# Summing the 32-wide squares of a causal channel attention on TensorE, by accumulating transposes

## The chip, the cores and the metric

The kernel runs on one core of a Trainium2 chip, in one launch. The metric is the device time of the whole launch in microseconds, as a median over runs.

## The reference, cut to what matters

The input x has 8 batches of 512 tokens with 256 features, all in 32-bit floats. Four layers follow each other, each with a layer norm ahead and a residual behind it: attention A, a feed-forward part, attention B (an ordinary causal attention over tokens) and the same feed-forward part again. The change lies in attention A, which attends, for each token and each of 16 heads, over the head's own 64 channels:

```python
Q = (x @ Wq + bq).reshape(b, s, H, C) * inv_sqrt_c      # H, C = 16, 64
K = (x @ Wk + bk).reshape(b, s, H, C)
V = (x @ Wv + bv).reshape(b, s, H, C)
scores = jnp.einsum('bshq,bshk->bshqk', Q, K)
mask = jnp.triu(jnp.ones((C, C), dtype=bool), 1)
scores = jnp.where(mask, -jnp.inf, scores)
w = jax.nn.softmax(scores, axis=-1)
attn = jnp.einsum('bshqk,bshk->bshq', w, V)
```

So for every token and head there is a lower triangle of 64 x 64 products q_i k_j, their exponentials, the sum of these over j (the denominator) and the sum of these times v_j (the numerator). None of this is a matmul over tokens: it is elementwise work with a token on each partition.

## The kernel before

**Squares.** A triangle of 64 is cut into one square of 32 x 32, two of 16, four of 8 and so on, and the diagonal. The kernel takes 128 tokens (i, of 4) of a batch (b, of 8) and 4 heads (g, of 4) at a time: 128 groups (b, g, i). The squares of a group are worked in four *units* (`units`, `NU = 4`): unit 0 has the squares of 32 of two heads, unit 2 those of the other two heads, unit 1 all squares of 16, and unit 3 all smaller ones. The loop runs over 512 *steps*, one unit each; `self.at(n - k)` names the unit that entered k steps ago, so a unit goes through a software pipeline of some ten steps.

**One unit's way.** `scores` (L804) forms the products of q and k: on POOL for units 0 and 2, on DVE for units 1 and 3. `exps` (L818, ACT) takes the exponential in place one step later. `weigh` (L828, DVE) multiplies by v into the other part of the same buffer, again one step later; so a buffer of 4096 columns holds 2048 exponentials (e) and 2048 weighted ones (ev). `halve` (L834) starts, from POOL's queue, a DMA that adds the upper 2048 columns onto the lower 2048. For the squares of 32 `fold` (L839, POOL) then adds 1024 columns onto 1024, `gather` (L865) reduces on DVE the remaining 8 columns of each row to one, and `add_rows` (L872, POOL) adds these 128 sums (e and ev of two squares, 32 rows each) to the accumulator `acc` of the group. Units 1 and 3 have no fold. Then `invert` (L876, DVE), `divide` (L880, POOL), `turn_group` (L888, PE transposes) and `project_out` (L896, PE) make the new x.

**Layout.** In `pieces` a buffer of unit 0 or 2 is laid out as (b a x i j): four blocks b of 8 columns, a for e or ev, x for the two squares, i for the 32 rows, and j, the 8 columns of a block, innermost. So each row's sum runs over neighbouring elements.

**Buffers.** The three buffers `w` of units 0 and 2 turn round. PSUM has eight banks; attention A has one of them, `bank`, in two halves of 256 columns, which `half_bank` hands out in turn to the transposes of x (L567), the product k (L761, copied away by L781), the transposed group (L888, copied by L738) and the output product (L896 to L491, copied by L907). q and v stay in another PSUM tile, `qv` (L766), from which DVE reads them.

**Order.** The order of PE, DVE, ACT and POOL is written out by hand: a step has three parts, and after each part the generator of the later layers (`after_a`: feed-forward L1072, L1140, L1166, attention B, feed-forward) of an earlier batch is advanced by as many pieces as the constant `total` allows. The engines run through their queues in program order. The later layers of the last batch remain when attention A is done; that is the tail.

These lines of `step` tell where the sums of a square of 32 are made, n being the present step:

```python
            b, i, g, u = self.at(n - 4)      # second part
            if u == 0:
                self.fold(b, i, g, u)
            b, i, g, u = self.at(n - 3)
            if u == 2:
                self.fold(b, i, g, u)
...
            b, i, g, u = self.at(n - 4)      # third part
            if u == 2:
                self.gather(b, i, g, u)
            b, i, g, u = self.at(n - 5)
            if u == 0:
                self.gather(b, i, g, u)
```

Of the kernel before, what the change touches and what calls it, by code (L numbers as in the profile page):

```python
# [16 lines left out]
P = 128  # L17
# [267 lines left out]
def fast_path(ctx: ExitStack, tc: tile.TileContext, k, t, flag):  # L285
# [214 lines left out]


    bank = ps_a.tile([P, 2, GW], F32, name="bank")
    halves = [0]

    def half_bank():
        halves[0] ^= 1
        return bank[:, halves[0], :]

    def judge():

# [72 lines left out]

    JB = 8

    def pieces(w, n, off, nsq, cols):

        def of_rows(v):
            return v[:, cols].rearrange("p (x t) -> p x t", t=2 * n)[:, :, n:]

        def of_cols(v):
            return v[:, cols].rearrange("p (x t) -> p x t", t=2 * n)[:, :, :n]

        if n < 16:
            e, ev = (
                w[:, a * SMALL + off : a * SMALL + off + nsq * n * n].rearrange("p (x i j) -> p x i j", i=n, j=n)  # L600
                for a in range(2)
            )
            yield e, ev, lambda v: of_rows(v).unsqueeze(3), lambda v: of_cols(v).unsqueeze(2)
            return
        both = w.rearrange("p (b a x i j) -> p a b x i j", a=2, x=nsq, i=n, j=JB)
        if n == 32:
            for x in range(nsq):
                yield (
                    both[:, 0, :, x],
                    both[:, 1, :, x],  # L610
                    lambda v, x=x: of_rows(v)[:, x].unsqueeze(1).unsqueeze(3),
                    lambda v, x=x: of_cols(v)[:, x].rearrange("p (b j) -> p b j", j=JB).unsqueeze(2),
                )
        else:
            for k in range(n // JB):
                yield (
                    both[:, 0, k],
                    both[:, 1, k],
                    lambda v: of_rows(v).unsqueeze(3),
                    lambda v, k=k: of_cols(v)[:, :, k * JB : (k + 1) * JB].unsqueeze(2),  # L620
                )

    class AttentionA:
# [33 lines left out]
        def step(self, n):  # L657

            weighed = self.at(n - 2)
            if weighed[0] is not None:  # L660
                self.weigh(*weighed)
            unit = self.at(n)
            on_pool = unit[3] in (0, 2)
            if on_pool:
                half = self.scores(*unit)
                next(half)
            if weighed[0] is not None:
                self.halve(*weighed)
            if on_pool:
                next(half, None)  # L670
            b, i, g, u = self.at(n + 40)
            if u == 0 and g == 0 and i == 0 and b > 0:
                self.x[b] = load_x(b)
            b, i, g, u = self.at(n + 10)
            if u == 0 and g == 0 and i == 0 and b > 0:
                self.measure(b)
            b, i, g, u = self.at(n + 8)
            if u == 0 and g == 0:
                self.live["xn"] = normed(self.x[b][:, i, :], *self.rn[b, i], "a")
            b, i, g, u = self.at(n - 5)  # L680
            if u == NU - 1:
                self.invert(b, i, g)
            b, i, g, u = self.at(n - 4)
            if u == 1:
                self.gather(b, i, g, u)
            b, i, g, u = self.at(n + 7)
            if u == 0 and g == 0:
                nc.scalar.copy(self.live[b, i], self.live.pop("ps_ln"))
            if self.at(n - 1)[0] is not None:
                self.exps(*self.at(n - 1))  # L690
            yield
            if unit[0] is not None and not on_pool:
                for _ in self.scores(*unit):
                    pass
            for args in self.sums:
                self.add_rows(*args)
            self.sums = []
            b, i, g, u = self.at(n - 5)
            if u == NU - 1:
                self.divide(b, i, g)  # L700
            b, i, g, u = self.at(n - 2)
            if u == NU - 1:
                self.small_squares(b, i, g)

            b, i, g, u = self.at(n - 4)
            if u == 0:
                self.fold(b, i, g, u)
            b, i, g, u = self.at(n - 3)
            if u == 2:
                self.fold(b, i, g, u)  # L710
            b, i, g, u = self.at(n - 9)
            if u == NU - 1:
                self.new_x(b, i, g)
            b, i, g, u = self.at(n + 2)
            if u == 0:
                self.keep_qk(b, i, g)
            b, i, g, u = self.at(n - 7)
            if u == NU - 1:
                self.turn_group(b, i, g)
            b, i, g, u = self.at(n - 8)  # L720
            if u == NU - 1:
                self.project_out(b, i, g)
            b, i, g, u = self.at(n + 3)
            if u == 0:
                self.project(b, i, g)
            yield
            b, i, g, u = self.at(n - 4)
            if u == 2:
                self.gather(b, i, g, u)
            b, i, g, u = self.at(n - 5)  # L730
            if u == 0:
                self.gather(b, i, g, u)
            b, i, g, u = self.at(n - 3)
            if u == NU - 1:
                self.gather(b, i, g, u)
            b, i, g, u = self.at(n - 7)
            if u == NU - 1:
                nc.scalar.copy(self.live["att"], self.live.pop("pta"))  # L738
            b, i, g, u = self.at(n + 8)
            if u == 0 and g == 0:  # L740
                self.live[b, i] = lnp.tile([P, DC, P], F32, tag="xnt_a", name=f"xnta_{b}_{i}", bufs=NT)
                self.live["ps_ln"] = turned_over(self.live.pop("xn"), half_bank().rearrange("p (c s) -> p c s", c=DC))
            yield

        def measure(self, b, tiles=range(NT)):
# [39 lines left out]
        def scores(self, b, i, g, n_u):  # L785

            qv, kt = self.live[b, i, g][:2]
            if n_u == 0:
                acc = ap_.tile([P, 2, GW], F32, tag="acc", name=f"acc_{b}_{i}_{g}", bufs=3)
                self.live[b, i, g].append(acc)  # L790
                nc.vector.tensor_tensor(acc[:, 0, :], qv[:, 0], kt[:, 0], ALU.mult)

            if n_u in (0, 2):
                w = wt.tile([P, 4096], F32, tag="w", name=f"w_{b}_{i}_{g}_{n_u}", bufs=3)
            elif n_u == 1:
                w = wt.tile([P, 4096], F32, tag="w16", name=f"w16_{b}_{i}_{g}")
            else:
                w = wt.tile([P, 2 * SMALL], F32, tag="ws", name=f"ws_{b}_{i}_{g}")
            self.live[b, i, g, n_u] = w
            eng, q = (nc.gpsimd, kt[:, 1]) if n_u in (0, 2) else (nc.vector, qv[:, 0])  # L800
            for n, off, nsq, cols in squares(units[n_u]):
                for e, ev, rows, columns in pieces(w, n, off, nsq, cols):
                    shape = list(e.shape)
                    eng.tensor_tensor(  # L804
                        e, rows(q).to_broadcast(shape), columns(kt[:, 0]).to_broadcast(shape), ALU.mult
                    )
                    yield

        def exps(self, b, i, g, n_u):
            w = self.live[b, i, g, n_u]  # L810
            if n_u == 0:
                acc = self.live[b, i, g][2]
                nc.scalar.activation(acc[:, 0, :], acc[:, 0, :], AF.Exp, scale=C**-0.5)
            if n_u < NU - 1:
                e = w.rearrange("p (b a r) -> p a b r", a=2, b=units[n_u][0][0] // JB)[:, 0]
            else:
                e = w[:, :SMALL]
            nc.scalar.activation(e, e, AF.Exp, scale=C**-0.5)  # L818
# [14 lines left out]
                w = self.live[b, i, g, n_u]  # L833
                nc.gpsimd.dma_start(w[:, :2048], w[:, 2048:], accum_op=ALU.add)  # L834

        def fold(self, b, i, g, n_u):

            w = self.live[b, i, g, n_u]
            nc.gpsimd.tensor_tensor(w[:, :1024], w[:, :1024], w[:, 1024:2048], ALU.add)  # L839

        def columns_of(self, w, n, off, nsq):

# [15 lines left out]
        def gather(self, b, i, g, n_u):  # L858


            w = self.live.pop((b, i, g, n_u))
            for n, off, nsq, cols in squares(units[n_u]):
                if n > 2:
                    red = ap_.tile([P, 2, nsq * n], F32, tag=f"red{nsq * n}", name=f"red_{b}_{i}_{g}_{n_u}_{n}", bufs=2 + (n < 32))
                    nc.vector.tensor_reduce(red, self.columns_of(w, n, off, nsq), AX.X, ALU.add)  # L865
                    self.sums.append((b, i, g, n, cols, red))

# [604 lines left out]
```

## Time and profile before

| what | value |
|---|---|
| time, median of 3 runs | 3989.1 us (3984.17 to 3989.51) |
| span of the profiled execution | 3990.8 us |
| PE, weight load (PEld) | 3039.9, 2055.2 us busy |
| DVE, ACT, POOL | 3375.9, 2341.3, 3077.9 us busy |
| DMA issues of `halve` | 384, 7.8 us median from issue to landing |
| mean granted TensorE clock | 0.849 |

The page gives no time of the profiled execution other than its span. The span lies 1.7 us above the median of the unprofiled runs, so the two are taken as one. Busy times are shares of work done, not of work that mattered; "idle before, releaser" in a group's row says how long the engine stood still just before these instructions and what ended that. POOL's DMA issues are not counted in its busy time. Weight loads overlap matmuls, and the ends of matmuls are modelled.

### The profile page before, as it was taken

Reading aid. Unit: us, or ns where it says so; the run is one execution under the profiler, and the core shown is the slowest. Engines: PE = TensorE matmul, PEld = TensorE weight load, DVE = VectorE, ACT = ScalarE, POOL = GpSimd, SP = SyncE. Lnnn points to the kernel's source line nnn. Section 1 sums busy time; section 2 is a strip of 40 time slices with the busy share of each in tenths; the row PEclk is TensorE's granted clock in tenths of the full one; section 3 lists DMA queues with packets and bytes.
Section 4 is the critical chain, followed back from the end, with each engine's and each line's share of the span. In section 5 each row is a group of like instructions: output and inputs, shape, how many; then the busy total and the mean of one; then the engine's idle time right before and its main releaser. Section 6 shows DMA issues by size and latency. Waiting matters only on the chain.

```text
span 3990.8 us, 37932 instructions
## 1 busy us (share of the span) xinstructions
PE 3039.9 (76%) x12464; PEld 2055.2 (52%) x12464; DVE 3375.9 (85%) x3776; ACT 2341.3 (59%) x3156; POOL 3077.9 (77%) x3040
## 2 busy tenths in 40 slices
PE   5653487687877878678876878778787778778988
PEld 2231264365634656356643656346553556446847
DVE  7999988998899888998899988998989888996115
ACT  3444475576665675666755766666755767565342
POOL 6888878887888788887788887887888877886111
PEclk7556599798987988888987989879898889879999
DMA  8766777577776877768775877668776677767304
GB/s 229 182 137 137 159 197 158 124 191 189 199 154 139 196 191 178 148 163 202 200 157 118 208 186 194 149 142 213 174 190 143 160 182 206 158 129 211 116 28 169
DMA packets 118346, 669.24 MB, mean 168 GB/s; under 512 B 12662, under 2 KB 31865, under 8 KB 43643
## 3 DMA queue, kind: packets, MB, share of 16 engines
q0 software_dynamic: 78336, 570.46, 63.2%
q1 hardware_dynamic: 39804, 96.27, 6.7%
q8 instruction: 101, 1.65, 0.2%
q14 instruction: 105, 0.86, 0.1%
HBM read 254.07 MB, written 9.96 MB: 66 GB/s over the span
## 4 chain that ended last, share of the span: by engine, by line
DVE 38%; PE 18%; POOL 14%; DMA 13%; ACT 8%; issue 8%; SPq 0%; ACTq 0%; POOLq 0%; DVEq 0%
DVE red L865 15%; DMA w<-w 13%; DVE w L828 10%; PE ph L1140 5%; ACT w L818 4%; POOL w L804 3%; POOL w L839 3%; DVE ws L828 3%; PE pqkb L1187 3%; POOL acc L872 3%; DVE w L804 2%; DVE ws L804 2%; POOL h L1056 2%; POOL w L834 2%; DVE acc L876 2%
## 5 line engine op out<-in xcount | busy, mean ns | idle before, releaser
L818 ACT ACTIVATE w<-w 128x2048 f32<-128x2048 f32 x384 | 733.8, 1912 | 659.2 <-POOL w L804 461.3
L1140 PE MATMUL ph<-h,hidden 128*128 128x512 f32 x4096 | 1042.9, 411 | 72.4 <-POOL h L1056 42.9
L804 POOL TENSOR_TENSOR w<-k 128x1024 f32<-128x1024 f32 x512 | 1077.4, 2104 | 7.7 <-ACT k L782 7.1
L1140 PEld LDWEIGHTS ph<-h,hidden 128*128 128x128 f32 x4096 | 792.3, 195 | 275.3 <-POOL h L1056 53.8
L828 DVE TENSOR_TENSOR w<-w,qv 128x1024 f32<-128x1024 f32 x768 | 898.8, 1211 | 22.4 <-ACT w L818 22.4
L865 DVE TENSOR_REDUCE red<-w 128x128 f32<-128x1024 f32 (+1 forms) x384 | 601.3, 1566 | 178.0 <-DMA w<-w 93.6
L839 POOL TENSOR_TENSOR w<-w 128x1024 f32<-128x1024 f32 x256 | 643.7, 2514 | 82.9 <-DMA w<-w 82.3
L834 POOL DMA_DIRECT2D w<-w x384 | 337.9, 880 | 349.0 <-issue 121.1
L872 POOL TENSOR_TENSOR acc<-acc,red 128x256 f32<-128x256 f32 (+1 forms) x640 | 471.2, 736 | 142.7 <-DVE red L865 122.0
L865 DVE TENSOR_REDUCE red<-ws 128x256 f32<-128x2048 f32 (+1 forms) x256 | 435.4, 1742 | 0.0
L766 PE MATMUL qv<-wqv,xnta 128*128 128x512 f32 x512 | 299.7, 716 | 104.6 <-DVE ws L828 95.4
L1072 PE MATMUL pw<-xnt,gate 128*128 128x512 f32 (+2 forms) x1152 | 301.8, 422 | 21.7 <-ACT silu L1048 16.1
L828 DVE TENSOR_TENSOR ws<-ws,qv 128x1024 f32<-128x1024 f32 (+3 forms) x512 | 294.3, 635 | 27.6 <-ACT ws L818 27.6
L804 DVE TENSOR_TENSOR w<-qv,k 128x1024 f32<-128x1024 f32 x256 | 301.1, 1218 | 3.6
L804 DVE TENSOR_TENSOR ws<-qv,k 128x1024 f32<-128x1024 f32 (+3 forms) x512 | 299.5, 646 | 0.2 <-issue 0.2
L888 PE MATMUL bank<-ident,acc 128*128 128x128 f32 x256 | 62.4, 333 | 284.5 <-ACT k L781 278.6
L818 ACT ACTIVATE ws<-ws 128x1920 f32<-128x1920 f32 x128 | 231.5, 1808 | 80.7 <-DVE ws L804 80.1
L1072 PEld LDWEIGHTS pw<-xnt,gate 128*128 128x128 f32 x1152 | 230.8, 215 | 76.2 <-ACT silu L1048 20.4
L1249 ACT ACTIVATE eb<-psb 128x256 f32<-128x256 f32 (+3 forms) x512 | 182.1, 443 | 139.1 <-PE psb L1246 138.6
L1166 PE MATMUL pof<-w,h 128*128 128x256 f32 x1024 | 244.9, 392 | 22.8 <-ACT h L1105 22.8
L1105 ACT ACTIVATE h<-ph,s_sb 128x512 fp32r<-128x512 f32 (+1 forms) x256 | 171.2, 688 | 151.1 <-PE ph L1140 149.7
L876 DVE RECIPROCAL acc<-acc 128x256 f32<-128x256 f32 x128 | 222.9, 1741 | 11.9 <-POOL acc L872 11.9
(149 smaller groups left out, 4846.4 us busy)
## 6 DMA issues: line engine op xcount, KB each, us to landing
w<-w POOLq DMA_DIRECT2D x384, 1024.0 KB, 7.8
hidden<-in_h POOLq DMA_DIRECT2D x128, 1024.0 KB, 7.9
gate<-in_w12p POOLq DMA_DIRECT2D x32, 1024.0 KB, 9.1
w<-w_d SPq DMA_DIRECT2D x16, 1024.0 KB, 11.5
wqv<-wqv_d SPq DMA_DIRECT2D x31, 512.0 KB, 4.6
wo<-in_wo SPq DMA_DIRECT2D x32, 256.0 KB, 7.6
wbqk<-wbqk_d SPq DMA_DIRECT2D x8, 1024.0 KB, 9.0
w<-in_h SPq DMA_DIRECT2D x8, 1024.0 KB, 8.6
```

The lines of the kernel that those rows point to most:

```text
L766: nc.tensor.matmul(qv.rearrange("p j f -> p (j f)"), xnt[:, c, :], wqv[:, c, :], start=(c == 0), stop=(c == DC - 1),)
L804: eng.tensor_tensor(e, rows(q).to_broadcast(shape), columns(kt[:, 0]).to_broadcast(shape), ALU.mult)
L818: nc.scalar.activation(e, e, AF.Exp, scale=C**-0.5)
L828: nc.vector.tensor_tensor(ev, e, columns(qv[:, 1]).to_broadcast(list(e.shape)), ALU.mult)
L834: nc.gpsimd.dma_start(w[:, :2048], w[:, 2048:], accum_op=ALU.add)
L839: nc.gpsimd.tensor_tensor(w[:, :1024], w[:, :1024], w[:, 1024:2048], ALU.add)
L865: nc.vector.tensor_reduce(red, self.columns_of(w, n, off, nsq), AX.X, ALU.add)
L872: nc.gpsimd.tensor_tensor(rows, rows, part.rearrange("p a (x i) -> p a x i", i=n), ALU.add)
L876: nc.vector.reciprocal(acc[:, 0, :], acc[:, 0, :])
L1072: nc.tensor.matmul(pj[:, toks], w[:, m % 4, j, c, :], xs[:, p, c, toks], start=(p == 0 and c == 0), stop=(p == 1 and c == DC - 1),)
L1140: nc.tensor.matmul(pss[j], w[:, j, c, :], h_in(p, c), start=(p == 0 and c == 0), stop=(p == 1 and c == MC - 1),)
L1166: nc.tensor.matmul(po, h(0, c)[:, i * P : (i + 1) * P], w3[:, c, :], start=(c == 0), stop=False)
```

## The change

The squares of 32 are laid out as (j a x i): the column j outermost, and within one column 128 numbers, e and ev of two squares with 32 rows each. The halving DMA still adds 2048 columns onto 2048, which now leaves 16 columns j of 128 numbers each. Instead of fold, reduction and addition on POOL, TensorE transposes these 16 blocks of 128 x 128 one after the other into the same 128 columns of PSUM, with accumulation (`turn_sums`), ACT copies the sum to SBUF (`keep_sums`), TensorE transposes it back (`turn_sums_back`), and DVE adds it from PSUM to `acc` (`add_sums`). The second half of `bank` is kept for this; all other users share the first half. POOL still makes the products in two instructions (`parts=2`), and DVE's weighting of such a unit is one instruction instead of two. The tiles `red` of all widths now have three buffers.

```diff
     bank = ps_a.tile([P, 2, GW], F32, name="bank")
-    halves = [0]
     def half_bank():
-        halves[0] ^= 1
-        return bank[:, halves[0], :]
+        return bank[:, 0, :]
...
-    def pieces(w, n, off, nsq, cols):
+    def pieces(w, n, off, nsq, cols, parts=1):
...
-        both = w.rearrange("p (b a x i j) -> p a b x i j", a=2, x=nsq, i=n, j=JB)
         if n == 32:
-            for x in range(nsq):
+            both = w.rearrange("p (j a x i) -> p a j x i", a=2, x=nsq, i=n)
+            step = n // parts
+            for k in range(0, n, step):
                 yield (
-                    both[:, 0, :, x],
-                    both[:, 1, :, x],
-                    lambda v, x=x: of_rows(v)[:, x].unsqueeze(1).unsqueeze(3),
-                    lambda v, x=x: of_cols(v)[:, x].rearrange("p (b j) -> p b j", j=JB).unsqueeze(2),
+                    both[:, 0, k : k + step],
+                    both[:, 1, k : k + step],
+                    lambda v: of_rows(v).unsqueeze(1),
+                    lambda v, k=k: of_cols(v)[:, :, k : k + step].rearrange("p x j -> p j x").unsqueeze(3),
                 )
...
+            if self.at(n - 5)[3] in (0, 2):      # first part, ahead of exps
+                self.keep_sums()
...
-            if u == 0:
-                self.fold(b, i, g, u)      # at(n - 4), second part
-            if u == 2:
-                self.fold(b, i, g, u)      # at(n - 3), second part
+            if self.at(n - 5)[3] in (0, 2):      # second part, after keep_qk, ahead of turn_group
+                self.turn_sums_back()
...
-            if u == 2:
-                self.gather(b, i, g, u)    # at(n - 4), third part
-            if u == 0:
-                self.gather(b, i, g, u)    # at(n - 5), third part
+            b, i, g, u = self.at(n - 5)          # third part
+            if u in (0, 2):
+                self.add_sums(b, i, g, u)
...
+            b, i, g, u = self.at(n - 4)          # third part, last
+            if u in (0, 2):
+                self.turn_sums(b, i, g, u)
...
+        def turn_sums(self, b, i, g, n_u):
+            w = self.live.pop((b, i, g, n_u))
+            for j in range(16):
+                nc.tensor.matmul(
+                    bank[:, 1, :P], w[:, j * P : (j + 1) * P], ident,
+                    start=(j == 0), stop=(j == 15), is_transpose=True,
+                )
+        def keep_sums(self):
+            self.live["sums"] = ap_.tile([P, P], F32, tag="sums", name="sums")
+            nc.scalar.copy(self.live["sums"], bank[:, 1, :P])
+        def turn_sums_back(self):
+            nc.tensor.transpose(bank[:, 1, P:], self.live.pop("sums"), ident)
+        def add_sums(self, b, i, g, n_u):
+            ((n, h0, nh),) = units[n_u]
+            acc = self.live[b, i, g][2]
+            rows = acc[:, :, h0 * C : (h0 + nh) * C].rearrange("p a (x t) -> p a x t", t=2 * n)[..., n:]
+            nc.vector.tensor_tensor(
+                rows, rows, bank[:, 1, P:].rearrange("p (a x i) -> p a x i", a=2, i=n), ALU.add
+            )
```

More of the change, by code (lines that the diff above doesn't have):

```diff
@@ L604, in pieces @@
             return
-        both = w.rearrange("p (b a x i j) -> p a b x i j", a=2, x=nsq, i=n, j=JB)
         if n == 32:
-            for x in range(nsq):
+            both = w.rearrange("p (j a x i) -> p a j x i", a=2, x=nsq, i=n)
+            step = n // parts
+            for k in range(0, n, step):
                 yield (
-                    both[:, 0, :, x],
-                    both[:, 1, :, x],
-                    lambda v, x=x: of_rows(v)[:, x].unsqueeze(1).unsqueeze(3),
-                    lambda v, x=x: of_cols(v)[:, x].rearrange("p (b j) -> p b j", j=JB).unsqueeze(2),
+                    both[:, 0, k : k + step],
+                    both[:, 1, k : k + step],
+                    lambda v: of_rows(v).unsqueeze(1),
+                    lambda v, k=k: of_cols(v)[:, :, k : k + step].rearrange("p x j -> p j x").unsqueeze(3),
                 )
         else:
+            both = w.rearrange("p (b a x i j) -> p a b x i j", a=2, x=nsq, i=n, j=JB)
             for k in range(n // JB):
@@ L703, in step @@
                 self.small_squares(b, i, g)
-            b, i, g, u = self.at(n - 4)
-            if u == 0:
-                self.fold(b, i, g, u)
-            b, i, g, u = self.at(n - 3)
-            if u == 2:
-                self.fold(b, i, g, u)
             b, i, g, u = self.at(n - 9)
@@ L726, in step @@
             yield
-            b, i, g, u = self.at(n - 4)
-            if u == 2:
-                self.gather(b, i, g, u)
             b, i, g, u = self.at(n - 5)
-            if u == 0:
-                self.gather(b, i, g, u)
+            if u in (0, 2):
+                self.add_sums(b, i, g, u)
             b, i, g, u = self.at(n - 3)
@@ L801, in scores @@
             for n, off, nsq, cols in squares(units[n_u]):
-                for e, ev, rows, columns in pieces(w, n, off, nsq, cols):
+                for e, ev, rows, columns in pieces(w, n, off, nsq, cols, parts=2):
                     shape = list(e.shape)
@@ L813, in exps @@
                 nc.scalar.activation(acc[:, 0, :], acc[:, 0, :], AF.Exp, scale=C**-0.5)
-            if n_u < NU - 1:
+            if n_u in (0, 2):
+                e = w.rearrange("p (j a r) -> p a j r", a=2, j=32)[:, 0]
+            elif n_u == 1:
                 e = w.rearrange("p (b a r) -> p a b r", a=2, b=units[n_u][0][0] // JB)[:, 0]
@@ L834, in halve @@
                 nc.gpsimd.dma_start(w[:, :2048], w[:, 2048:], accum_op=ALU.add)
-        def fold(self, b, i, g, n_u):
-            w = self.live[b, i, g, n_u]
-            nc.gpsimd.tensor_tensor(w[:, :1024], w[:, :1024], w[:, 1024:2048], ALU.add)
+        def turn_sums(self, b, i, g, n_u):
+            w = self.live.pop((b, i, g, n_u))
+            for j in range(16):
+                nc.tensor.matmul(
+                    bank[:, 1, :P],
+                    w[:, j * P : (j + 1) * P],
+                    ident,
+                    start=(j == 0),
+                    stop=(j == 15),
+                    is_transpose=True,
+                )
[11 more added lines that the diff above has]
+            )
         def columns_of(self, w, n, off, nsq):
@@ L863, in gather @@
                 if n > 2:
-                    red = ap_.tile([P, 2, nsq * n], F32, tag=f"red{nsq * n}", name=f"red_{b}_{i}_{g}_{n_u}_{n}", bufs=2 + (n < 32))
+                    red = ap_.tile([P, 2, nsq * n], F32, tag=f"red{nsq * n}", name=f"red_{b}_{i}_{g}_{n_u}_{n}", bufs=3)
                     nc.vector.tensor_reduce(red, self.columns_of(w, n, off, nsq), AX.X, ALU.add)
```

## The prediction

> **What bounds the kernel now.** I read the busy shares and the chain of the page first, then windows cut at phase borders, then the waits inside one slow group, then the groups of the lines that the change touches.
>
> ```profile
> PE 3039.9 (76%) x12464; PEld 2055.2 (52%) x12464; DVE 3375.9 (85%) x3776; ACT 2341.3 (59%) x3156; POOL 3077.9 (77%) x3040
> ...
> DVE 38%; PE 18%; POOL 14%; DMA 13%; ACT 8%; issue 8%; SPq 0%; ACTq 0%; POOLq 0%; DVEq 0%
> ```
>
> VectorE leads both rows, but a share is a mean over phases. The starts of L791 (one per group of four steps, 128 in all) give a time per group: 23.7 us in the start-up, 24 to 26 while attention B runs, 26 to 35 while a feed-forward part runs. Cut there (start-up, eleven feed-forward groups, five attention-B groups, tail):
>
> ```profile
> 36.00:458.00 422.00, 215.62 (x443) 109.09 (x443) 409.25 (x423) 173.00 (x186) 358.55 (x313) 0.57 0.73 161
> ...
> 1233.70:1570.10 336.40, 270.33 (x1051) 203.47 (x1050) 294.27 (x343) 221.12 (x266) 272.70 (x278) 0.89 0.76 183
> 1570.10:1698.80 128.70, 94.89 (x488) 46.86 (x487) 120.25 (x125) 77.20 (x132) 110.77 (x99) 0.84 0.69 147
> ...
> 3618.00:3991.00 373.00, 339.70 (x1595) 254.41 (x1593) 126.44 (x154) 138.66 (x252) 89.46 (x125) 0.96 0.40 130
> ```
>
> Columns: length, then busy us of PE, weight load, DVE, ACT, POOL, then clock, DMA share, GB/s. DVE fills 97% of the start-up and 93% of attention B: it is the bound there. In the feed-forward stretch it is 87%, PE 80%, POOL 81%: nobody is full, so a loop of waits costs some 42 us of DVE idleness. The tail has no attention A left and is PE's. One feed-forward group (1512 to 1544) shows the loop:
>
> ```profile
> POOL w L839 <- DMA w<-w: 6.0, 1, 6.0
> DVE red L865 <- POOL w L839: 5.5, 1, 5.5
> ```
>
> The `fold` of unit 2 stands one step after its halving DMA; where feed-forward weights load too, the DMA is late, POOL stands at the fold, and DVE at the reduction behind it. Over the execution DVE waits 84.1 us for L839 and 93.6 us for DMA directly (unit 1's reduction, which the change leaves).
>
> **What the Trainium skill says.** "TensorE: Matmul & The Clock Gate", Part 4, says that a transpose is a matmul against identity, about 275 ns in a kernel, and that the clock gate does not open for it as for other matmuls. Lengths agree (L888: 270 to 449 ns); whether sixteen in a row hold the clock down no trace here shows. The same page, Part 2, says that only weight loads are pulled ahead, matmuls stay in program order: so a waiting transpose holds all feed-forward work behind it. "PSUM — Partial Sum Buffer", Terms, says that two engines may not be in one bank and quadrant at once. The trace agrees that the bank is guarded as a whole: L888 waits 278.6 us for the copy L781, which reads the other half.
>
> **The change, part by part.** Prices, per instruction:
>
> ```profile
> L839 POOL TENSOR_TENSOR w<-w 128x1024 f32<-128x1024 f32 x256 | 643.7, 2514 | 82.9 <-DMA w<-w 82.3 <-DVE red L865 0.3
> L865 DVE TENSOR_REDUCE red<-w 128x128 f32<-128x1024 f32 x256 | 309.5, 1209 | 84.2 <-POOL w L839 84.1
> L872 POOL TENSOR_TENSOR acc<-acc,red 128x128 f32<-128x128 f32 x256 | 179.6, 702 | 0.3 <-DVE red L865 0.3
> ```
> ```profile
> 1499.70 0.41 PE L888 MATMUL bank<-ident,acc 128*128 128x128 f32 x2 [2.95 <-ACT k L781]
> 1499.87 8.24 PE L1140 MATMUL ph<-h,hidden 128*128 128x512 f32 x28
> ...
> 3544.05 0.66 PEld L1312 LDWEIGHTS pytb<-ident,ytb 128*128 128x128 f32 x3 [0.20 <-issue]
> ```
>
> *POOL, per group:* two folds (5.03 us) and two additions (1.40) go: -6.43. Its products L804 keep their number, with the broadcast now innermost in the other operand; no row shows that form, so I bound it by the shortest and longest of today's (1.94 and 2.59 us) and take 2.1, no change. Four of them cost at most 2 us more, hidden under the 6.43 just freed. The halving DMAs stay at 384, on the same queue.
>
> *DVE, per group:* two reductions go (-2.42). The weighting L828 becomes one instruction of 2048 instead of two of 1.211: the reduction of 2048 takes 2.28, so -0.14 each, bounds 0 and -0.14: -0.28. Two additions from PSUM come, priced by the 128x128 product with a PSUM operand (L804, 0.279): +0.56. Sum **-2.15**.
>
> *ACT, per group:* two copies of 128x128; the 256-wide copy takes 0.37, so at most +0.74. ACT idles over 7 us per group: no cost by itself. But each copy stands ahead of the exponentials of its step, and these, then DVE's weighting, wait if TensorE is late. The exponentials keep their size, in runs of 64 (price unknown; 1.9 us today; a tenth more is still hidden).
>
> *PE, per group:* 32 accumulating transposes and 2 back. In the timeline two transposes hold PE for 1499.87 - 1499.70 = 0.17 us, but loads are then partly ahead; starts of consecutive transposes in the trace are mostly 0.11 us apart at full clock. At half clock three loads take 0.66 us, the last 0.23 of them: (0.66-0.23)/2 = 0.22 apart. So 34 x 0.11 = **+3.7 us**, bound 34 x 0.22 = 7.5. They run beside DVE's work, not on its path, while PE has idle time.
>
> *Waits.* `turn_sums` stands 2 2/3 steps after the halving is issued (some 19 us; landings 7.8 median, 18.0 longest), so DMA seldom holds it. It waits on the bank for ACT's `att` copy; `turn_sums_back` waits for `keep_sums`; `add_sums` waits for both PE and POOL's last addition to `acc`. Queued behind: feed-forward matmuls on PE, exponentials on ACT, the next weighting on DVE. Each has about one third of a step. Using one half for everything else costs nothing, because the halves already exclude each other (above); without that cover it could cost PE up to the 2.2 us per group that L888 waits now. A `w` buffer is freed by PE a step earlier than DVE's reduction freed it.
>
> *Start-up*, 17 groups: DVE was the bound and stays it; PE at half clock goes from 12.7 to 20 us of 21.5. Gain 17 x 2.15 = 37, I take 35.
> *Attention B*, seven times five groups of 128.7: the first of the five is PE-bound, four gain 2: 8 x 7 = 56.
> *Feed-forward*, about 75 groups, 336.4 per eleven: DVE could give 23.6 plus some 10 of the vanished fold waits, floor 303. PE needs 270.3 + 11 x 3.7 = 311 without one idle microsecond. PE is therefore what is late next; it idles 66 us today, and I leave it 6: 317, gain 19.4, or 1.8 per group: 75 x 1.8 = 135.
> *Tail:* same work, 0.
>
> Sum 35 + 56 + 135 = 226. The profiled span is 3990.8, 1.7 above the median of 3989.1, so the sum can be taken from the latter: 3763, rounded to **3760**.
>
> **Rivals.**
> *DVE keeps the pace.* PE's own figure includes half-clock work (clock 0.89), and a denser PE may run at full clock. Then all 128 groups give 2.15 and the 84 us of fold waits go: 3989 - 275 - 84 = 3630. For it: ACT and PE wait for each other more than they work late. Against: the 311.
>
> *DMA keeps the feed-forward stretches as they are.* Its share is 0.76 there, and DVE already waits for it at L865. Only 35 + 56 remain: 3900. Against: most of the stall is the early fold.
>
> *Slower: the transposes run at half clock and TensorE becomes the bound at the bank.* A stretch then needs 270.3 + 11 x 7.5 = 353 plus the 6 of idleness, 359 against 336.4: +22.6 per eleven, 75/11 x 22.6 = +154; attention B comes to 94.9 + 37 = 132 against 128.7, +3 x 7 = 21; the start-up still gives 35. 3989 + 154 + 21 - 35 = 4129. It decides from a spacing of (336.4 - 6 - 270.3)/374 = 0.16 us; less if DVE stands at `add_sums`. For it: the skill's sentence and the waits in step order. Against: around the transposes lie ordinary matmuls, which kept the clock at 0.89.
>
> **How the numbers follow.** Likeliest case 0.50 (3660 to 3850), DVE pace 0.20, DMA 0.09, slower 0.21. Two runs differ from no change if over 0.2% (8 us) apart. Nearly all of the first three are faster: 0.77; between the cases 0.03 same; 0.20 slower. The range runs from a little under the DVE case to just past no change, which leaves out most of the slower case: 3610 to 4030.
>
> **What would show it.** Right: L839 gone, 256 fewer reductions, start-up groups at 21.5, transposes 0.11 apart, feed-forward stretches near 317 with PE over 93% busy. Wrong: transposes near 0.2 apart, a lower clock, DVE waiting for PE at the new addition or ACT at the new copy by more than 2 us per group, or POOL's L804 well over 2.6.

## The result, and the profile after

The changed kernel takes 4062.6 us (4058.8 to 4063.8) against 3989.3: a ratio of 1.018, with a 95% interval of 1.017 to 1.019. It is **slower by 73 us**, outside the range of the prediction. The profiled execution has a span of 4062.0.

The page's first part and its chain:

```profile
PE 3380.7 (83%) x16816; PEld 2511.3 (62%) x16816; DVE 3141.0 (77%) x3520; ACT 2387.0 (59%) x3412; POOL 2390.8 (59%) x2528
...
PE 52%; ACT 20%; DVE 15%; issue 6%; POOL 4%; DMA 3%; ACTq 0%; SPq 0%; POOLq 0%; DVEq 0%
```

DVE lost 235 us of work and POOL 687, as intended, PE gained 341, and no engine is over 83%. (Contrary to what is said above, POOL's busy time does contain its DMA issues: L834 has 337.9 us before and 339.7 after, so the difference hardly changes.) Yet the time rose. The chain tells where to look: DVE's part fell from 38% to 15%, and PE and ACT together now hold 72%. The same stages as before the change (start-up, eleven feed-forward groups, five attention-B groups, tail; the columns are length, then busy PE, PEld, DVE, ACT, POOL, then clock, DMA share, GB/s):

```profile
35.70:451.70 416.00, 254.56 (x1029) 181.34 (x1030) 376.48 (x389) 178.67 (x219) 269.67 (x245) 0.78 0.74 163
1244.80:1578.40 333.60, 299.65 (x1432) 237.91 (x1431) 274.12 (x322) 227.99 (x293) 217.61 (x240) 0.95 0.76 185
1578.40:1722.80 144.40, 108.56 (x652) 67.64 (x651) 111.10 (x116) 75.73 (x138) 79.87 (x73) 0.85 0.61 132
3691.00:4062.00 371.00, 343.70 (x1656) 259.34 (x1653) 122.21 (x152) 137.90 (x254) 75.17 (x113) 0.97 0.39 130
```

The tail is as it was. The feed-forward stretch is 3 us shorter; over five such stretches the two traces have 1672.6 and 1666.9. The start-up gained 6 us where DVE lost 33 us of work. And attention B, where now nobody is short of time, is the loser: 144.4 us instead of 128.7, and 714.3 instead of 646.6 over five stretches. DVE fills 77% of it, PE 75%.

The groups of the new instructions (op, tiles, count, then busy us and mean ns, then the idle time just before them and what ended it):

```profile
L840 PE MATMUL bank<-ident,w 128*128 128x128 f32 x4096 | 629.2, 319 | 180.9 <-ACT x L933 118.2 <-ACT att L733 55.2 <-DMA w<-w 5.8
...
L863 DVE TENSOR_TENSOR acc<-acc,bank 128x128 f32<-128x128 f32 x256 | 73.3, 286 | 394.5 <-PE bank L491 217.8 <-POOL acc L898 99.7 <-PE bank L759 46.3
L852 ACT COPY sums<-bank 128x128 f32<-128x128 f32 x256 | 69.1, 270 | 468.1 <-PE bank L840 468.1
```

The right-hand sides carry the result. DVE stands 394.5 us at an addition whose own work is 73; ACT stands 468.1 us at the copy; PE stands 180.9 us at the transposes, waiting for ACT to empty the bank. These instructions are new, and their waits with them. A piece of attention B's timeline (start, length, instruction, idle time before it and its releaser) shows how they hang together:

```profile
1609.08 0.40 ACT L933 COPY x<-bank 128x256 f32<-128x256 f32 x1
...
1609.53 3.27 PE L840 MATMUL bank<-ident,w 128*128 128x128 f32 x16 [3.94 <-ACT x L933]
...
1614.92 1.64 ACT L1275 ACTIVATE eb<-psb 128x384 f32<-128x384 f32 x4 [5.44 <-PE psb L1272]
...
1616.41 0.30 ACT L852 COPY sums<-bank 128x128 f32<-128x128 f32 x1
...
1616.77 0.33 PE L856 MATMUL bank<-ident,sums 128*128 128x128 f32 x1 [1.78 <-ACT sums L852]
...
1618.10 0.29 DVE L863 TENSOR_TENSOR acc<-acc,bank 128x128 f32<-128x128 f32 x1 [1.92 <-PE bank L759]
```

PE idles 3.94 us because its next instruction, the first transpose, may not enter the bank before ACT has copied x out of it; that copy stands behind exponentials in ACT's queue. Only after the sixteen transposes does PE reach attention B's scores, so ACT idles 5.44 us for them; behind those exponentials stands the copy of the sums; so PE waits 1.78 us for it, and DVE 1.92 us for PE, in the end for the k product L759 in the other half of the bank. One late engine makes the next one late, round and round. At the second unit DVE waits 6.26 us:

```profile
1633.55 0.28 PE L856 MATMUL bank<-ident,sums 128*128 128x128 f32 x1
...
1634.54 0.59 PE L491 MATMUL bank<-x,ident 128*128 128x256 f32 x2
...
1635.27 0.29 DVE L863 TENSOR_TENSOR acc<-acc,bank 128x128 f32<-128x128 f32 x1 [6.26 <-PE bank L491]
```

The sums were back at 1633.83, but the output product into the other half of the same bank stood next in PE's order, and the addition waited for that too, until 1635.13. Over the execution DVE stands at the addition 264 us for PE (217.8 and 46.3). Set against the end of each unit's own L856, 133 us of these pass before the sums are back in PSUM, and 131 us after it, while only the other half of the bank is still being written (the ends of matmuls are modelled).

### The profile page after: what moved, and what is told of

It reads as the page before. It is cut to its first block, busy times and chain, and to the rows that moved or that the text cites. A ratio compares the mean times of both kernels' runs of the same rounds, so it can differ in the third digit from the quotient of the medians.

```text
span 4062.0 us, 46555 instructions
## 1 busy us (share of the span) xinstructions
PE 3380.7 (83%) x16816; PEld 2511.3 (62%) x16816; DVE 3141.0 (77%) x3520; ACT 2387.0 (59%) x3412; POOL 2390.8 (59%) x2528
## 4 chain that ended last, share of the span: by engine, by line
PE 52%; ACT 20%; DVE 15%; issue 6%; POOL 4%; DMA 3%; ACTq 0%; SPq 0%; POOLq 0%; DVEq 0%
PE ph L1166 13%; PE bank L840 11%; ACT w L818 6%; PE pof L1192 4%; DVE w L828 4%; PE pw L1098 4%; DVE red L891 3%; PE pyb L1280 3%; PE qv L764 3%; PE pqkb L1213 3%; DMA w<-w 3%; DVE ws L828 2%; ACT eb L1275 2%; PE psb L1268 2%; PE bank L922 2%
## 5 line engine op out<-in xcount | busy, mean ns | idle before, releaser
L1166 PE MATMUL ph<-h,hidden 128*128 128x512 f32 x4096 | 1022.5, 404 | 22.0 <-POOL h L1082 21.5
L828 DVE TENSOR_TENSOR w<-w,qv 128x2048 f32<-128x2048 f32 (+1 forms) x512 | 883.5, 1747 | 14.1 <-ACT w L818 12.8
L1166 PEld LDWEIGHTS ph<-h,hidden 128*128 128x128 f32 x4096 | 767.8, 190 | 199.3 <-POOL h L1082 24.7
L834 POOL DMA_DIRECT2D w<-w x384 | 339.7, 885 | 905.6 <-DVE w L828 475.9
L840 PE MATMUL bank<-ident,w 128*128 128x128 f32 x4096 | 629.2, 319 | 180.9 <-ACT x L933 118.2
L840 PEld LDWEIGHTS bank<-ident,w 128*128 128x128 f32 x4096 | 576.4, 167 | 240.8 <-ACT x L933 131.6
L898 POOL TENSOR_TENSOR acc<-acc,red 128x256 f32<-128x256 f32 x384 | 311.5, 811 | 396.1 <-DVE red L891 386.1
L863 DVE TENSOR_TENSOR acc<-acc,bank 128x128 f32<-128x128 f32 x256 | 73.3, 286 | 394.5 <-PE bank L491 217.8
L852 ACT COPY sums<-bank 128x128 f32<-128x128 f32 x256 | 69.1, 270 | 468.1 <-PE bank L840 468.1
L891 DVE TENSOR_REDUCE red<-w 128x256 f32<-128x2048 f32 x128 | 291.8, 2280 | 34.7 <-DMA w<-w 34.7
L764 PE MATMUL qv<-wqv,xnta 128*128 128x512 f32 x512 | 250.3, 613 | 8.7 <-DVE ws L828 7.0
```

What stands on the lines that cost most here:

```text
L764: nc.tensor.matmul(qv.rearrange("p j f -> p (j f)"), xnt[:, c, :], wqv[:, c, :], start=(c == 0), stop=(c == DC - 1),)
L828: nc.vector.tensor_tensor(ev, e, columns(qv[:, 1]).to_broadcast(list(e.shape)), ALU.mult)
L840: nc.tensor.matmul(bank[:, 1, :P], w[:, j * P : (j + 1) * P], ident, start=(j == 0), stop=(j == 15), is_transpose=True,)
L898: nc.gpsimd.tensor_tensor(rows, rows, part.rearrange("p a (x i) -> p a x i", i=n), ALU.add)
L1166: nc.tensor.matmul(pss[j], w[:, j, c, :], h_in(p, c), start=(p == 0 and c == 0), stop=(p == 1 and c == MC - 1),)
```

## The experiments

Two theories. **A:** TensorE has too little time for 4352 more instructions. **B:** the work fits, but the way of the sums (PE to ACT to PE to DVE) hands over too often, through one bank, at places in the queues where somebody always waits. All ratios are to the kernel before.

**One transpose of sixteen.**

```diff
-            for j in range(16):
+            for j in range(1):
...
-                    stop=(j == 15),
+                    stop=True,
```

> The changed kernel, with one of the sixteen accumulating transposes of each unit; the other fifteen blocks are left out of the sums. All waits, copies, the transpose back and the addition stay. Theory A (TensorE has too little time: 629 us of L840 are too many): PE loses some 550 us of work, the kernel comes below the one before, 3700 to 3800. Theory B (the hand-overs PE to ACT to PE to DVE through one bank, each within a third of a step, cost more than the saved work): most of the loss stays, 3950 to 4050, DVE still waits over 250 us at the addition.

Measured 3904.1, ratio 0.979 (0.977 to 0.982). Fifteen transposes per unit cost 159 us, less than A said and more than B said, so A is not nothing: 76 of them lie in the five feed-forward stretches, where PE is 90% busy. But even with hardly any new work on PE the kernel was 144 us above the 3760 that I had forecast for all of it. DVE still stood 139.6 us for L491, 136.2 for POOL's additions and 22.0 for L759 at its addition: 298 us.

**No way back.**

```diff
-                self.keep_sums()
...
-                self.turn_sums_back()
...
-                self.add_sums(b, i, g, u)
```

> The changed kernel with all sixteen transposes, but without the copy to SBUF, the transpose back and DVE's addition: the sums of the 32-wide squares are left out of acc. Theory A (TensorE's time): still 4000 to 4060. Theory B (hand-overs): DVE loses its 395 us of waits at the addition and ACT its 468 us at the copy, 3650 to 3780.

Measured 3841.5, ratio 0.963 (0.962 to 0.965), between the two expectations and nearer to B's. The way back costs **221 us**. That is as much as its instructions' own work added up (L852 69.1, L863 73.3, L856 78.2), though this work is spread over three engines that all had idle time. PE is at 86% here, more than in the changed kernel, in 230 us less: its time was not the limit there. PE still waits at the transposes (L833 in this run), mostly for ACT's copy of x:

```profile
L833 PE MATMUL bank<-ident,w 128*128 128x128 f32 x4096 | 625.2, 318 | 161.4 <-ACT x L926 79.4
```

The start-up's 17 groups take 374.8 us, 22.0 each.

**One half of the bank, in the kernel before.**

```diff
-        halves[0] ^= 1
-        return bank[:, halves[0], :]
+        return bank[:, 0, :]
```

> The kernel before, with half_bank always giving the first half. Both theories of the prediction and after: no change, 3989 within 8 us, since the halves already exclude each other. If giving up the second half is what costs: 4020 to 4060.

Measured 3988.0, ratio 1.000 (0.999 to 1.001). Giving up the second half costs nothing in the kernel before, as predicted.

**Transposes one part earlier, ACT's copy behind the exponentials.**

```diff
             if u == 0:
                 self.project(b, i, g)
+            b, i, g, u = self.at(n - 4)      # end of the second part
+            if u in (0, 2):
+                self.turn_sums(b, i, g, u)
...
-            if self.at(n - 5)[3] in (0, 2):  # first part
-                self.keep_sums()
...
-            b, i, g, u = self.at(n - 4)      # third part, last
-            if u in (0, 2):
-                self.turn_sums(b, i, g, u)
+            if self.at(n - 4)[3] in (0, 2):  # end of the third part
+                self.keep_sums()
```

> The changed kernel with the sixteen transposes at the end of the second part of the step instead of the third, and ACT's copy at the end of that third part instead of the first part of the next step, so that it no longer stands ahead of the exponentials. Theory A: no change, 4040 to 4080. Theory B, if the copy on ACT is the costly hand-over: 3900 to 4000. If DVE's wait at the addition is the costly one: 4030 to 4070, with the wait at the addition as long as before.

Measured 3977.3, ratio 0.997 (0.996 to 0.998): 85 us better, for the same instructions, as B said. That speaks against A. The wait of ACT at the copy fell from 468 to 365 us (276 for the sixteen transposes, 89 for the transposes of x, L565) and that of DVE for L491 from 218 to 167, though the addition had not moved: the waits are linked. Two others grew: PE's for x from 118 to 193 us, and ACT's at the copy of att from 49 to 245.

**The addition one part later.**

```diff
-            b, i, g, u = self.at(n - 5)      # third part
+            b, i, g, u = self.at(n - 6)      # first part of the next step, ahead of invert
             if u in (0, 2):
                 self.add_sums(b, i, g, u)
```

> The changed kernel with DVE's addition one part later: in the first part of the next step, after the weighting and just ahead of the reciprocal that needs it, instead of at the end of its step. Theory B1 (of the 221 us that the return way costs, DVE standing at the addition for TensorE, 264 us in the profile, and for POOL, 100 us, is the larger part): 3880 to 3960, start-up group 22.0 instead of 24.5 us. Theory B2 (the copy on ACT and the transpose back on PE are the larger part): 4020 to 4060.

Measured 4007.1, ratio 1.004 (1.003 to 1.006), between both expectations: 55 us better. The start-up did nearly what B1 said (384.3 us for 17 groups instead of 416.0, or 22.6 each), so there the waits at the addition were the loss. Elsewhere the wait only moved. DVE's longest wait is now one instruction away, at the weighting behind ACT:

```profile
DVE w L828 <- ACT w L818: 216.4, 99, 5.8
```

**No addition, but copy and transpose back.**

```diff
-            if u in (0, 2):
-                self.add_sums(b, i, g, u)
```

> The changed kernel with the copy on ACT and the transpose back, but without DVE's addition: the sums of the 32-wide squares are left out of acc. B1: 3850 to 3900, near the run without any way back (3841.5). B2: 4000 to 4060. The difference to that earlier run is the price of copy and transpose back alone.

Measured 3978.0, ratio 0.997 (0.996 to 0.998). It parts the 221 us, taken out in this order: 85 belong to the addition, 136 to the copy and the transpose back. That is neither B1 nor B2 pure: both halves of the way back cost, and B2's is the larger.

**Both moves.** The two diffs above together.

> Transposes one part earlier, ACT's copy after the exponentials, DVE's addition one part later, all together. If the 85 us of the early transposes and the gain of the late addition come from different waits they add: 3820 to 3900. If both relieve the same wait: not more than 20 us under the better of the two.

Measured 3964.2, ratio 0.994 (0.992 to 0.995), 13 us under the better of the two. The moves relieve mostly the same loop. PE still waits 206 us at L840 for ACT's copy of x.

**POOL folds once more, eight transposes remain** (on top of the late addition).

```diff
+            b, i, g, u = self.at(n - 4)      # second part
+            if u in (0, 2):
+                self.fold(b, i, g, u)
...
-            for j in range(16):
+            for j in range(8):
...
-                    stop=(j == 15),
+                    stop=(j == 7),
```

> The late addition, and POOL, which idles over a third of the time in the changed kernel, folds 2048 columns onto 1024 again (in the second part, four steps after the unit entered, for both units), so that eight transposes instead of sixteen remain. Half of the 159 us that fifteen transposes cost: about 80 us below the late addition alone if TensorE's time still binds; no gain or a loss if the fold's wait for the DMA on POOL, which delays the products, takes its place.

Measured 4347.4, ratio 1.089 (1.087 to 1.091): a clear miss, 340 us worse than without the fold, though it takes work off PE and POOL is busy only 69%.

```profile
PE bank L848 <- POOL w L842: 622.7, 168, 8.0
```

POOL didn't wait for the DMA, which I had feared: the trace has no idle time of POOL before any fold (L842). The fold stands behind POOL's products and behind the next halving, whose issue waits for DVE (294 us at the addition, 248 at the weighting), and PE stands at the first transpose until it is through, with the feed-forward work behind it. A hand-over from a fourth engine cost more than half the transposes were worth.

**Transposes first in the step.** The same instructions as in the changed kernel, each where its predecessor was meant to be done. Only the new places are shown; the old ones are gone.

```diff
         def step(self, n):
+            b, i, g, u = self.at(n - 4)      # very first
+            if u in (0, 2):
+                self.turn_sums(b, i, g, u)
...
+            b, i, g, u = self.at(n - 5)      # first part, behind the weighting
+            if u in (0, 2):
+                self.add_sums(b, i, g, u)
...
+            if self.at(n - 4)[3] in (0, 2):  # second part, behind new_x and keep_qk
+                self.keep_sums()
...
+            if self.at(n - 4)[3] in (0, 2):  # end of the third part
+                self.turn_sums_back()
```

> The changed kernel with the same instructions in other places, chosen so that no hand-over through the bank waits in a queue: the sixteen transposes at the very start of the step four after the unit entered (ahead of ACT's copies out of the bank, two steps after the halving DMA was issued), ACT's copy in the second part behind new_x and keep_qk, the transpose back at the end of the third part, DVE's addition in the first part of the next step after the weighting. Theory B (placing, not amount of work): PE's waits for ACT at L840, 174 us in the changed kernel, go, and the time falls below the best so far (3964), to 3800 to 3920; the start-up group stays near 22.5 us. Theory A (what is left is TensorE's time): 3940 to 3990. If the DMA's landing is now what PE waits for: over 3990.

Measured 3898.5 (3891.0 to 3904.4), ratio 0.977 (0.975 to 0.980): **164 us below the changed kernel and 91 below the one before**, with no instruction taken away, as theory B said. The start-up groups take 23.2 us, a little more than the 22.5 expected. Its stretches of the same eleven and five groups:

```profile
1196.50:1523.80 327.30, 296.72 (x1417) 235.44 (x1416) 273.61 (x321) 228.65 (x294) 215.70 (x240) 0.95 0.77 188
1523.80:1646.60 122.80, 97.89 (x666) 60.19 (x666) 110.38 (x115) 77.25 (x138) 81.33 (x74) 0.93 0.72 155
```

Attention B takes 122.8 us instead of 144.4. Work on DVE and ACT is nearly that of the changed kernel. PE's is 10.7 us less there, at a granted clock of 0.93 instead of 0.85; shorter waits and a higher clock come together, and no run separates them. In this order no copy of ACT's stands between PE's last write into the bank and the transposes, so PE hardly waits for ACT there:

```profile
L840 PE MATMUL bank<-ident,w 128*128 128x128 f32 x4096 | 527.4, 286 | 49.5 <-DMA w<-w 31.8
```

ACT's copies of x and k now wait for PE instead (176.7 and 120.6 us). What is left: DVE stands at the addition for the transpose back.

```profile
DVE acc L863 <- PE bank L856: 231.6, 85, 8.1
```

**The same without the way back.** Copy, transpose back and addition left out of the last order.

> The order with the transposes first (3898.5), without copy, transpose back and addition: the sums of the 32-wide squares are left out of acc. In the changed kernel this way back cost 221 us. Theory B (placing): in the new order most of that is gone, 3820 to 3870, so the way back costs 30 to 80 us, of which some 40 are the additions' own work on DVE. Theory A (amount of work): as before, some 220 us, 3680.

Measured 3769.5, ratio 0.945 (0.943 to 0.947). In the better order the way back costs 129 us instead of 221: between the two expectations. So the better order takes 92 us off the price of the way back, and gains another 72 without it (3841.5 to 3769.5). Here the landing of the halving DMA begins to count: PE waits 133.4 us for it at the transposes.

**The addition at the end of that step.** The order above with the addition where the changed kernel has it.

> The order with the transposes first, but DVE's addition at the end of the same step's third part, where the changed kernel has it; TensorE then has two parts more for the transpose back, but the output product or the next k product writes the bank in between, and the addition waits for that too, and for POOL's additions to acc. If the 231 us that DVE stands at the addition for L856 come from its early place: 3840 to 3890. If the bank and POOL matter more: 3910 to 3950.

Measured 3944.1, ratio 0.988 (0.985 to 0.990), 46 us worse than with the early addition, as said for the case that the bank and POOL matter more. DVE stands at the addition 181 us for PE, and 164 of them pass after the unit's own sums are back, while the other half of the bank is still being written; POOL's additions cost another 122.

A bank of its own for the sums was not tried: attention B has five tiles of `ps_f` at once (four of scores, one of values), which with two of `qv` and one `bank` are all eight that the kernel has. So the shares of the common bank and of the hand-overs as such in the 221 us stay open; the 131 and 164 us above show that the bank's is not small. The last order moved four things at once, and of these only the addition was moved back alone.

## Why the prediction was wrong, step by step

**The failed step** is the paragraph on waits, and the sentence that two copies on ACT are "no cost by itself". I listed whom each hand-over would hold up, gave each "about one third of a step", and entered zero. That failed in two places. The table has the stages in us, from the starts of the first product of each group (L791 in the kernel before, L789 in the changed one):

| kernel | start-up, 17 groups | five feed-forward stretches | five of attention B |
|---|---|---|---|
| before | 421.7 | 1672.6 | 646.6 |
| changed | 416.0 | 1666.9 | 714.3 |
| changed, one transpose of sixteen | 409.6 | 1590.5 | 671.6 |
| changed, no way back | 374.8 | 1562.4 | 684.1 |
| transposes first | 394.8 | 1633.9 | 625.4 |
| transposes first, no way back | 375.2 | 1596.8 | 595.5 |

*The way back.* It cost 221 us, mostly in the start-up (41.2 in the table) and the feed-forward stretches (104.5 in these five), where it ate the forecast gain. One third of a step is no slack where the producer is itself waiting in its own queue: L852 stood 1.8 us on average at every copy (468.1/256), and L863 1.5 us at every addition (394.5/256). The latter is 3.1 us per group on DVE, more than the 2.15 I had it save. ACT's wait at the copy is 3.7 us per group and DVE's for PE at the addition 2.1, both above the 2 us that the prediction named as a sign of being wrong.

*The place of the transposes.* In attention B the way back is only 30 of the 68 us lost; 37 stay without it. In these five stretches PE stood at the transposes 45 us for ACT's copy of x and 20 for that of att with the way back (L840), and 49 and 20 without it. With one transpose of sixteen 25 us of the loss are left, so the amount of work counts too, where it stands behind such a wait. But with all sixteen first in the step these waits are gone, and so is the whole loss (625.4).

The sum for the rest was not right as it stood: without the way back, and so without the additions that the sum had priced, the kernel takes 3841.5 instead of 3760. Only with both, no way back and the better order, does it come to 3769.5, with 119 us per stretch of attention B against the forecast 121 and 319 per feed-forward stretch against 317.

*The bank.* I saw in the profile before that its halves exclude each other, drew from it that giving up one half costs nothing, and was right on that (one half: 1.000). I did not draw the other conclusion: that new users of the bank would wait for all its old ones. I named ACT's copy of att (55.2 us at L840), but not that of x (118.2), and for L863 not the output product (217.8) in the other half.

*Start-up.* Forecast -35 us, measured -6. PE's share was put at 20 us per group and came to 15.0, at a clock of 0.78 instead of 0.57; there was room, as I said. The loss was a ping-pong on `acc` that I mentioned and did not price: POOL's additions end 0.7 to 0.8 us too late for DVE's, twice per group; with the late addition the start-up took 384.3 us.

*Attention B.* Forecast -8 per stretch, measured +14 (714.3 - 646.6 over five). I had called it DVE's and given PE's work away for nothing. But it is a chain of short hand-overs between PE (scores, values) and ACT (exponentials); a wait of PE there delays ACT, whatever their shares. ACT's wait for the scores, in the first of these stretches, before, in the changed kernel, and with the transposes first:

```profile
ACT eb L1249 <- PE psb L1246: 18.4, 10, 3.8
ACT eb L1275 <- PE psb L1272: 31.0, 13, 6.1
ACT eb L1275 <- PE psb L1272: 20.3, 16, 2.5
```

*Feed-forward.* Forecast 317 with PE at 311; measured 333.6 with PE at 300. PE's work was priced a little high (its clock rose from 0.89 to 0.95), the 6 us of idleness far too low: 34 us remain. The stall of the early fold did go, as forecast, and new ones took its place; POOL now waits for DVE at L834 instead.

*DVE's work.* Forecast -2.15 per group, measured -1.84 (235/128). Two weightings of 1.21 in a row took 2.34, not 2.42, since they overlap in the record; one of 2048 takes 2.28. The addition took 0.286, priced 0.279.

*POOL.* Its products in the new layout took 2.12 us against 2.10: right. Its busy time fell by 5.4 us per group (687/128), not by 6.43, as its records overlap in part.

*PE's spacing.* Forecast 0.11. The trace has a median of 0.109, and 29% of the gaps between transposes at 0.21; the mean is 0.144. That is below the 0.16 from which the rival at half clock would have decided. Its price of 4129 came nearer to the measured time than mine, by another mechanism. The reading that consecutive transposes are "mostly 0.11 us apart at full clock" in the profile before was partly luck: it holds for the fours of L1312 (0.109 in the median), while the pairs of L888 are 0.136 apart.

*The other rivals.* DMA: the transposes waited 5.8 us for the halving in all, and DVE's direct wait for DMA fell from 93.6 to 34.7: out, though the feed-forward stretches did stay nearly as they were. DVE keeps the pace: DVE is busy 77% and stands at the addition: out.

## What to carry to other kernels

Moving work to an engine with idle time is free only if nobody has to wait for the result; count the hand-overs between in-order queues, and look at the wait that the nearest existing one shows (here L888, 2.2 us per group) before you enter zero. In this kernel the engines wait for each other at a shared PSUM bank even where they use different halves, so try a producer ahead of the copies that empty the bank, not behind them. Compare stage by stage: here the way back cost most in the start-up and the feed-forward stretches, the place of the transposes in attention B. The same 4352 added TensorE instructions gave +1.8% or -2.3% by their place alone.

## What the runs showed of the hardware that I had not expected

Sixteen 32-bit transposes into the same columns of PSUM with accumulation follow each other at the pace of transposes into columns of their own (L1312 in the kernel before): 0.109 us from start to start in the median at full clock and 0.213 at half clock, for both.

The sentence of the Trainium skill that the prediction cites ("TensorE: Matmul & The Clock Gate", Part 4) had made me fear that they hold the clock down. The runs show the opposite: the mean granted clock rose from 0.849 to 0.907, and in the start-up from 0.57 to 0.78. With one transpose of sixteen and all else alike it is 0.855, and 0.60 in the start-up.
